# Moving a shared expert's first products into an attention loop's last steps, with the loads reordered and the results written by rows

## The chip, the cores and the metric

One Trainium2 chip, one of its cores. The time is device microseconds of one execution. Engines: PE is TensorE (PEld its weight loads), DVE is VectorE, ACT is ScalarE, POOL is GpSimd, SP is SyncE, which issues most DMAs.

## What is computed

A Perceiver layer in float32: cross attention from 32 x 64 latent rows to 32 x 1601 context rows, a span attention among the 64 rows, and a feed-forward with a shared expert and hashed experts. All residual.

```python
x = x + xattn(layernorm(x), ctx, ctx, mask)     # (32, 64, 256), 16 heads of 16, 1601 keys
x = x + span_attn(layernorm(x))                 # scores = -softplus(s1) * (pos - 64*sigmoid(s0))**2
x = x + ffn(layernorm(x))

# ffn, xf of (2048, 256)
shared = silu(xf @ sw1 + sb1) * (xf @ sw3 + sb3) @ sw2 + sb2      # 256 -> 512 -> 256
for k in range(2):                                                # two experts a row
    exp_ids = (arange(2048) * 11 + k * 7919) % 8                  # fixed by the row's number
    out += gelu(xf @ w1[e] + b1[e]) @ w2[e] + b2[e]               # 256 -> 256 -> 256
y = (shared + out / 2) / 2
```

The expert of a row depends on its number modulo 8 alone, so rows are treated in 8 classes `r`, each with two known experts.

## The kernel before

**Half batches.** The loop runs over 64 half batches `n`: batch `b = n // 2`, and half `c` of the heads. For each, TensorE makes scores `psc` (L454) in four groups of key chunks, VectorE adds the mask and puts them into `prob` (L463), and VectorE keeps a running maximum `mrun` in PSUM (L484). The maxima are turned by TensorE (`pm`, L491), reduced (`mc`, L498), turned back (`pb`, L506) and copied by ScalarE (`mb`, L510). GpSimd subtracts them from each of four pairs of heads (`less_maxima`, L515), ScalarE takes the exponential (L520), TensorE multiplies with the values into `pvs` (`values`, L530). `prob` has five slots, so that one half batch's scores are written while the last one's are read. Half batch `n` makes the scores of `n + 1`, and the projections of keys and values of the next batch (`pk` L419, `pv` L435) fill TensorE in between. In the last two half batches, 62 and 63, there is no next batch to project, and in 63 no next scores.

**The tile's steps.** Two batches make a tile of 128 rows. After its attention, `finish_steps` divides by the sums (`pr`, `rin`, `oT`), and `span_steps` does the output product `po`, the span attention and the norm ahead of the feed-forward. Its steps are taken out of an `agenda`, one in each of the loop's stretches: norm, transposes `tr_h`, `psp` and `pval`, the polynomial that ends in `mean` and `soft`, `sc` minus `mean` (L258), square, times `soft` (L263), minus `least` (L267), exponential, by `total` (L273), transposes `psa` (L281) copied to `aT`, products `po2` and `po3`, norm, and the transposed rows `xfT` (L312), from which all of the feed-forward reads. `x_kept` keeps the rows in DRAM for the last addition.

**Order.** PE, DVE, ACT and POOL run the loop in the order of the program (`manual_schedule`). What comes after `order.close()` is ordered by the scheduler, and its instructions can be put among the loop's last ones. SP and the DMAs it issues are ordered by the scheduler too. Every engine runs its instructions in order, and an instruction that waits holds those behind it. `mm_bank` hands out six PSUM banks in turn.

**The feed-forward.** After the loop the pools of the attention are closed, and the weights are loaded into their memory (L685). The shared expert's first products `p1`, `p3` (L725) run over four quarters of the rows by four chunks of the hidden width: 16 units of 8 matmul instructions each, with a Silu on ScalarE (L729) and the gated product on VectorE (L730). The last tile's steps run among the first 12; quarter 3 needs that tile. Then, class by class, `expert_hidden` makes `ph` (L748) and Gelu, and `expert_out` sums shared and expert terms in `py` (L766), with channels on the partitions. Biases are added as columns (`yT`, L770). At the end `yT` is transposed back (`pf`, L783), `x` is added (L785), and 16 tiles are stored (L786).

Of the kernel before, what the change touches and what calls it, by code (L numbers as in the profile page):

```python
# [53 lines left out]
B_2 = B_1 + 2 * E  # L54
B_S2 = B_2 + TOPK * 2 * E
B_V = B_S2 + 2
# [22 lines left out]
def perceiver_kernel(ctx: ExitStack, tc: tile.TileContext, a: dict[str, bass.AP], out: bass.AP):  # L79
# [13 lines left out]

    def mm_bank(name: str):
        return ps_mm.tile([P, 512], F32, tag="mm", name=name)
# [3 lines left out]
    nc.sync.dma_start(out=cst, in_=a["consts"])  # L99
# [6 lines left out]
    nc.sync.dma_start(out=cols, in_=a["cols"])  # L106
# [11 lines left out]
    load_x(0)  # L118

    def load_square(name: str, width: int = D):  # L120
        w = const.tile([P, 2, width], F32, name=f"{name}_sb")
        nc.scalar.dma_start(out=w, in_=a[name].rearrange("(c p) o -> p c o", p=P))
        return w

    wqT, wkT, wvT = (load_square(n) for n in ("wqT", "wkT", "wvT"))
    bo_row = const.tile([P, D], F32, name="bo_row")
    nc.scalar.dma_start(out=bo_row, in_=a["bo"].partition_broadcast(P))
    woP = const.tile([P, 4, D], F32, name="woP_sb")
    nc.scalar.dma_start(out=woP, in_=a["woP"])
    wspanT = load_square("wspanT", 2 * H)  # L130
    wvalT = load_square("wvalT")
    woutT = load_square("woutT")

# [183 lines left out]
    xattn = ExitStack()  # L317
    big = xattn.enter_context(tc.tile_pool(name="big", bufs=2))
# [7 lines left out]
    with tc.tile_pool(name="mask8", bufs=1) as mp:  # L326
        m8 = mp.tile([P, NKC, S], U8, name="m8")
        nc.sync.dma_start(out=m8[:CHUNK], in_=a["maskT"])
        nc.vector.tensor_scalar(madd[:CHUNK], m8[:CHUNK], -MASKED, MASKED, ALU.mult, ALU.add)
        nc.vector.tensor_scalar(  # L330
            madd[:CHUNK, NKC - 1, :], madd[:CHUNK, NKC - 1, :], cst[:CHUNK, C_PAD : C_PAD + 1],
            None, ALU.add,
        )
# [3 lines left out]
    prob = big.tile([P, 5, 2, NKC, P], F32, name="prob", bufs=1)  # L337
# [29 lines left out]
    cts: dict[int, list] = {}  # L367
# [31 lines left out]
    def load_context(b: int):  # L399
        cts[b] = []  # L400
        for g, (c0, n) in enumerate(GROUPS):
            k0, kn = c0 * CHUNK, min(n * CHUNK, KEYS - c0 * CHUNK)
            ct = big.tile([P, 2, 4 * CHUNK], F32, tag="ct", bufs=5, name=f"ct_{b}_{g}")
            nc.sync.dma_start(
                out=ct[:, :, :kn],
                in_=a["ctxT"][b].rearrange("(c p) k -> p c k", p=P)[:, :, k0 : k0 + kn],
            )
            cts[b].append(ct)
        if b % 2 == 0 and b // 2 + 1 < NTILE:
            t = b // 2 + 1  # L410
            load_x(t)
# [101 lines left out]
    def less_maxima(n: int, j: int, m):  # L513
        sj = pair_of(n, j)
        nc.gpsimd.tensor_tensor(  # L515
            sj, sj, m[:CHUNK, j, None, :].to_broadcast([CHUNK, NKC, P]), ALU.subtract
        )
# [4 lines left out]
    def values(n: int, r: int):  # L522
# [3 lines left out]
        for k in range(NKC):  # L526
            kn = min(CHUNK, KEYS - k * CHUNK)
            for j in range(4):
# [6 lines left out]
                )  # L535

# [43 lines left out]
    load_context(0)  # L580
    queries = query_steps(0)
    for _ in range(4):
        next(queries)
    for g in range(len(GROUPS)):
        project_keys(0, 0, g)
    for g in range(len(GROUPS)):
        scores(0, g, BETWEEN[g])
        if g == 0:
            first_maxima(0)
        project_keys(0, 1, g)  # L590
# [14 lines left out]
    for n, (b, c) in enumerate(halves):  # L605
# [12 lines left out]
        for g in range(len(GROUPS)):  # L618
            if g == 0:
# [13 lines left out]
            if g == 0:  # L633
                project(project_keys, c, 0)
                m = maxima_along_rows(turned[1])
                if n:
# [16 lines left out]
            less_maxima(n, g, m)  # L653
            run(4 * n + g)
            if g == 0 and n < last:
                first_maxima(n + 1)
# [12 lines left out]
    run(stretch)  # L669
    stretch += 1  # L670
# [7 lines left out]
    ps_mm = ctx.enter_context(tc.tile_pool(name="ps_mm", bufs=3, **psum))  # L678
    aside = mm_bank
    ps_y = ctx.enter_context(tc.tile_pool(name="ps_y", bufs=2, **psum))  # L680
    ps_h = ctx.enter_context(tc.tile_pool(name="ps_h", bufs=3, **psum))
# [6 lines left out]
    sw1 = load_weights("sw1_sb", 2, HS, a["sw1"])  # L688
    sw3 = load_weights("sw3_sb", 2, HS, a["sw3"])
    gT = ffn.tile([P, NHC, E, CL], F32, name="gT")  # L690
    sw2 = load_weights("sw2_sb", NHC, D, a["sw2"])
    w1, w2 = [], []
    for e in range(E):
        w1.append(load_weights(f"w1_{e}", 2, D, a["w1"][e]))
        w2.append(load_weights(f"w2_{e}", 2, D, a["w2"][e]))

    nc.gpsimd.tensor_tensor(sw2, sw2, sw2, ALU.add)
    ybias = ffn.tile([P, 2 * E], F32, name="ybias")
    nc.vector.tensor_tensor(
        ybias, cols[:, B_2 : B_2 + 2 * E], cols[:, B_2 + 2 * E : B_2 + 4 * E], ALU.add  # L700
    )
    for c in range(2):
        for _ in range(2):
            nc.vector.tensor_scalar(
                ybias[:, c * E : (c + 1) * E], ybias[:, c * E : (c + 1) * E],
                cols[:, B_S2 + c : B_S2 + c + 1], None, ALU.add,
            )
    nc.vector.tensor_scalar(ybias, ybias, 0.25, None, ALU.mult)

    QL = CL // 4
    for quarter in range(4):
        at = slice(quarter * QL, (quarter + 1) * QL)
        if quarter == 3:
            while agenda:
                run(stretch)
                stretch += 1
        for hc in range(NHC):
            hs = slice(hc * P, (hc + 1) * P)  # L720
            p1 = ps_h.tile([P, E, QL], F32, tag="h", name=f"p1_{quarter}_{hc}")
            p3 = ps_h.tile([P, E, QL], F32, tag="h", name=f"p3_{quarter}_{hc}")
            for ps, w in ((p1, sw1), (p3, sw3)):
                for c in range(2):
                    nc.tensor.matmul(  # L725
                        ps, lhsT=w[:, c, hs], rhs=xfT[:, c, :, at], start=(c == 0), stop=(c == 1)
                    )
            act = hid.tile([P, E, QL], F32, tag="act", name=f"act_{quarter}_{hc}")
            nc.scalar.activation(act, p1, AF.Silu, bias=cols[:, B_S1 + hc : B_S1 + hc + 1])  # L729
            nc.vector.scalar_tensor_tensor(  # L730
                gT[:, hc, :, at], p3, cols[:, B_S3 + hc : B_S3 + hc + 1], act, ALU.add, ALU.mult
            )
            run(stretch)
            stretch += 1

    yT = ffn.tile([P, 2, NT], F32, name="yT")
    xe = ffn.tile([P, NTILE, D], F32, name="xe")
    nc.sync.dma_start(out=xe, in_=x_kept.rearrange("t p d -> p t d"))
    yTr = yT.rearrange("p c (i r) -> p c r i", r=E)
# [19 lines left out]
    def expert_out(r: int, hids):  # L759
        py = ps_y.tile([P, 2, CL], F32, tag="y", name=f"py_{r}")  # L760
        for m in range(2):
            ms = slice(m * P, (m + 1) * P)
            terms = [(sw2[:, hc, ms], gT[:, hc, r, :]) for hc in range(NHC)]
            terms += [(w2[e][:, c, ms], hT[:, c, :]) for e, hT in hids for c in range(2)]
            for n, (w, x) in enumerate(terms):
                nc.tensor.matmul(  # L766
# [85 lines left out]
```

## Time and profile before

| | |
|---|---|
| median of 3 runs | 1680.48 us (1679.57 to 1681.05) |
| the profiled execution | 1680.07 us |
| its span, first to last instruction | 1678.3 us |
| mean granted TensorE clock | 0.988 |
| busy: PE, DVE, ACT, POOL | 1585.9, 1305.6, 911.3, 1105.9 us |

How to read it: all times in a view count from the start of the span. A window line gives the length, then busy microseconds and instructions of each engine, the granted TensorE clock, the share of the DMA engines and GB/s. A timeline line gives start, duration, engine, line, operation, out<-in, shape, count, and in brackets how long the engine had stood idle and what released it; several like instructions in a row are one line. A float32 matmul of the program is two instructions in these counts.

### The profile page before, as it was taken

How to read it: one execution, taken by the hardware profiler on the slowest of the kernel's cores; microseconds unless marked ns; L12 is line 12 of the kernel's file. 1: busy time of each engine (PE TensorE's matmuls, PEld its weight loads, DVE VectorE, ACT ScalarE, POOL GpSimd, SP SyncE). 2: the span in 40 equal slices, each digit the busy share in tenths (PEclk: the TensorE clock that was granted, in tenths of full speed). 3: DMA queues.
4: the chain of work that ended last, by engine and by line, in shares of the span. 5: the costliest groups of instructions: out<-in, count | busy, mean ns of one | idle time of the engine just before them, and what ended most of it. 6: DMA issues, size and time to landing. Idle time of an engine off the chain costs nothing.

```text
span 1678.3 us, 55766 instructions
## 1 busy us (share of the span) xinstructions
PE 1585.9 (94%) x25160; PEld 1192.8 (71%) x25160; DVE 1305.6 (78%) x2637; ACT 911.3 (54%) x1271; POOL 1105.9 (66%) x395
## 2 busy tenths in 40 slices
PE   6999999999999999999999999999999999859998
PEld 4777777777777777777777777777777777644586
DVE  4788988887888889888888888897889888873112
ACT  2555656565656656565656666555656565534210
POOL 0767767787686877677877868786768777672000
PEclk9999999999999999999999999999999999969999
DMA  4211111111111111111111111111111111003101
GB/s 131 58 40 42 33 40 40 38 42 48 41 42 47 41 36 33 41 39 38 41 48 41 42 48 41 39 38 39 37 43 32 45 42 32 2 26 117 54 0 51
DMA packets 51789, 72.50 MB, mean 43 GB/s; under 512 B 3684, under 2 KB 50912, under 8 KB 51552
## 3 DMA queue, kind: packets, MB, share of 16 engines
q1 hardware_dynamic: 49632, 66.95, 13.9%
q8 instruction: 197, 3.23, 0.8%
q10 hardware_dynamic: 1920, 2.00, 0.3%
q14 instruction: 40, 0.33, 0.1%
HBM read 64.74 MB, written 4.19 MB: 41 GB/s over the span
## 4 chain that ended last, share of the span: by engine, by line
PE 55%; DVE 38%; issue 3%; POOL 1%; DMA 1%; ACT 1%; POOLq 0%; ACTq 0%; DVEq 0%
DVE prob L463 13%; DVE mrun L484 13%; PE pk L419 12%; PE pv L435 12%; PE pvs L530 9%; PE psc L454 8%; PE py L766 3%; DVE rin L557 3%; PE p L725 2%; PE pm L491 2%; PE ph L748 2%; PE pb L506 1%; DVE least L266 1%; DVE mrun L251 1%; DVE total L271 1%
## 5 line engine op out<-in xcount | busy, mean ns | idle before, releaser
L515 POOL TENSOR_TENSOR prob<-prob,mb 124x1664 f32<-124x1664 f32 x256 | 950.3, 3731 | 330.4 <-ACT mb L510 330.4
L463 DVE TENSOR_TENSOR prob<-psc,madd 124x384 f32<-124x384 f32 (+1 forms) x1024 | 584.5, 584 | 188.7 <-PE psc L454 188.7
L484 DVE TENSOR_TENSOR mrun<-prob,mrun 124x512 f32<-124x512 f32 x704 | 484.1, 688 | 7.2 <-ACT mrun L476 4.3
L419 PE MATMUL pk<-ct,wkT_sb 128*128 128x372 f32 (+2 forms) x1024 | 406.1, 520 | 8.7 <-DVE prob L463 0.2
L520 ACT ACTIVATE prob<-prob 124x1664 f32<-124x1664 f32 x256 | 400.0, 1587 | 14.7 <-POOL prob L515 14.3
L435 PE MATMUL pv<-wvT_sb,ct 128*124 128x256 f32 (+1 forms) x1664 | 384.6, 379 | 0.0
L435 PEld LDWEIGHTS pv<-wvT_sb,ct 128*124 128x124 f32 (+1 forms) x1664 | 309.9, 186 | 77.3 <-DVE prob L463 2.4
L454 PE MATMUL psc<-qbd,kT 32*124 32x128 f32 x6656 | 298.5, 287 | 33.8 <-DVE prob L463 29.0
L423 ACT ACTIVATE kT<-pk,cols 128x372 f32<-128x372 f32 (+2 forms) x256 | 152.1, 594 | 293.8 <-PE pk L419 293.4
L454 PEld LDWEIGHTS psc<-qbd,kT 32*124 32x124 f32 x6656 | 235.3, 182 | 107.1 <-DVE prob L463 55.5
L419 PEld LDWEIGHTS pk<-ct,wkT_sb 128*128 128x128 f32 x1024 | 174.3, 190 | 112.0 <-issue 29.6
L441 ACT COPY v<-pv 124x512 f32<-124x512 f32 (+1 forms) x224 | 124.7, 557 | 215.4 <-PE pv L435 214.1
L530 PE MATMUL pvs<-prob,v 124*17 124x64 f32 x13312 | 216.0, 222 | 3.7 <-ACT prob L520 3.7
L530 PEld LDWEIGHTS pvs<-prob,v 124*17 124x17 f32 x13312 | 193.2, 99 | 29.4 <-issue 24.8
L770 DVE TENSOR_SCALAR yT<-py,ybias 128x256 f32<-128x256 f32 x16 | 10.9, 679 | 74.1 <-PE py L766 74.1
L725 PE MATMUL p<-xfT,sw_sb 128*128 128x512 f32 x128 | 58.7, 616 | 2.8 <-DMA sw_sb<-in_sw 1.4
L557 DVE RECIPROCAL rin<-pr 128x256 f32<-128x256 f32 x32 | 56.0, 1750 | 5.8 <-PE pr L553 5.8
L506 PEld LDWEIGHTS pb<-cst,mc 128*124 128x124 f32 x256 | 29.8, 135 | 35.9 <-DVE mc L498 30.1
L491 PE MATMUL pm<-cst,mx 124*128 124x124 f32 x256 | 40.7, 282 | 9.8 <-DVE mx L484 8.9
L725 PEld LDWEIGHTS p<-xfT,sw_sb 128*128 128x128 f32 x128 | 24.9, 198 | 33.8 <-issue 28.4
L484 DVE TENSOR_TENSOR mx<-prob,mrun 124x512 f32<-124x512 f32 x64 | 44.0, 687 | 2.2
L156 POOL TENSOR_TENSOR rstd_f<-ve_f,neghalf 128x1 f32<-128x1 f32 x16 | 8.8, 549 | 55.4 <-DVE ve_f L154 55.4
(138 smaller groups left out, 1224.7 us busy)
## 6 DMA issues: line engine op xcount, KB each, us to landing
ct<-in_ctxT SPq DMA_DIRECT2D x64, 372.0 KB, 3.2
ct<-in_ctxT SPq DMA_DIRECT2D x32, 496.0 KB, 3.6
ct<-in_ctxT SPq DMA_DIRECT2D x32, 361.0 KB, 3.1
w<-in_w SPq DMA_DIRECT2D x16, 256.0 KB, 7.1
x<-in_x SPq DMA_DIRECT2D x16, 128.0 KB, 2.0
x_kept<-x SPq DMA_DIRECT2D x16, 128.0 KB, 1.7
xe<-x_kept SPq DMA_DIRECT2D x1, 2048.0 KB, 8.2
out<-ot SPq DMA_DIRECT2D x16, 128.0 KB, 1.8
```

Of the source, the lines that this page charges most:

```text
L419: nc.tensor.matmul(ps[:, :kn], lhsT=wkT[:, i, c * P : (c + 1) * P], rhs=cts[b][g][:, i, :kn], start=(i == 0), stop=(i == 1),)
L423: nc.scalar.activation(kTs[c][:, k0 : k0 + kn], ps[:, :kn], AF.Identity, bias=cols[:, B_K + c : B_K + c + 1])
L435: nc.tensor.matmul(ps[:kn, n * D : (n + 1) * D], lhsT=cts[b][g][:, i, k0 : k0 + kn], rhs=wvT[:, i, :], start=(i == 0), stop=(i == 1),)
L441: nc.scalar.copy(vs[b % 2][:kn, 2 * u : 2 * u + n, :, :DK], ps[:kn, : n * D].rearrange("p (n h d) -> p n h d", n=n, d=DK),)
L454: nc.tensor.matmul(ps[:CHUNK, k * P : (k + 1) * P], lhsT=kTs[c][32 * j : 32 * j + 32, at : at + CHUNK], rhs=qbd[b // 2][32 * j : 32 * j + ...
L463: nc.vector.tensor_tensor(pair_of(n, j)[:, c0 : c0 + nb, :].rearrange("p k (e q) -> p k e q", e=2), ps[:CHUNK, : nb * P].rearrange("p (k e ...
L484: nc.vector.tensor_tensor(dst, block_of(n, k), run, ALU.max)
L515: nc.gpsimd.tensor_tensor(sj, sj, m[:CHUNK, j, None, :].to_broadcast([CHUNK, NKC, P]), ALU.subtract)
L520: nc.scalar.activation(pair_of(n, j), pair_of(n, j), AF.Exp)
L530: nc.tensor.matmul(pvs[32 * j : 32 * j + DK + 1, c, r, :], lhsT=v[:kn, k, 8 * c + h, :], rhs=pair_of(n, h // 2)[:kn, k, (h % 2) * S : (h % ...
L557: nc.vector.reciprocal(rin, pr[:, : 4 * S])
L725: nc.tensor.matmul(ps, lhsT=w[:, c, hs], rhs=xfT[:, c, :, at], start=(c == 0), stop=(c == 1))
```

## The change

- The first loads change places: on the ACT queue `wkT`, `wqT`, `wvT` alone; on SP the first piece of context, `x`, the constants, and the other pieces, with all other weights behind. `sw1` and `sw3` are loaded here too and stay. The program makes the four key products in turn with the query's steps.
- `prob` moves to a pool that is kept, and gated products, biases and residual rows of the feed-forward lie in its slots.
- A `unit` (two products, 8 matmul instructions) and its `gate` (Silu, gated product) are functions now. Units 0 to 2 run in half batch 62, 3 and 4 in 63, 5 to 11 among the last tile's steps, 12 to 15 after them.
- In half batch 63 `less_maxima` runs on VectorE instead of GpSimd.
- The second products have rows on the partitions: `py` takes the gated or hidden values as the stationary operand and the weights as the moving one. Biases come as rows: `b2row`, broadcast to all partitions, is summed into `brow` and from there into the residual rows `xe[r]`, by GpSimd. `yT`, the transposes and `ybias` go. Each `py` has one VectorE instruction and one store of 128 rows, eight apart.

```diff
+    wkT = load_square("wkT", nc.scalar)
+    load_piece(0, 0)
     load_x(0)
-    wqT, wkT, wvT = (load_square(n) for n in ("wqT", "wkT", "wvT"))
+    nc.sync.dma_start(out=cst, in_=a["consts"])
+    nc.sync.dma_start(out=cols, in_=a["cols"])
+    wqT = load_square("wqT", nc.scalar)
+    load_piece(0, 1)
+    load_piece(0, 2)
+    wvT = load_square("wvT", nc.scalar)
+    m8 = big.tile([P, NKC, S], U8, name="m8", bufs=1)
+    nc.sync.dma_start(out=m8[:CHUNK], in_=a["maskT"])
+    load_piece(0, 3)
...
+    woutT = load_square("woutT", nc.sync)
+    sw1 = load_square("sw1", nc.sync, HS)
+    sw3 = load_square("sw3", nc.sync, HS)
+    load_x(1)
...
-    def less_maxima(n: int, j: int, m):
+    def less_maxima(n: int, j: int, m, engine):
         sj = pair_of(n, j)
-        nc.gpsimd.tensor_tensor(
+        engine.tensor_tensor(
...
+    spare = prob.rearrange("p a b k q -> p a (b k q)")
+    REGION = E * 2 * QL
+
+    def region(h: int, hc: int):
+        a0, n = ((3, hc), (4, hc))[h] if hc < 3 else (0, h)
+        return spare[:, a0, n * REGION : (n + 1) * REGION].rearrange("p (r i) -> p r i", r=E)
...
+    def unit(u: int):
+        quarter, hc = divmod(u, NHC)
+        slot = slice(quarter * QL, (quarter + 1) * QL)
+        pair = []
+        for name, w in (("p1", sw1), ("p3", sw3)):
+            ps = mm_bank(f"{name}_{u}")
+            for c in range(2):
+                nc.tensor.matmul(
+                    ps, lhsT=w[:, c, hc * P : (hc + 1) * P], rhs=xfT[:, c, :, slot],
+                    start=(c == 0), stop=(c == 1),
+                )
+            pair.append(ps)
+        waiting.append((u, *pair))
+
+    def gate():
+        u, p1, p3 = waiting.popleft()
...
+        nc.scalar.activation(act, p1, AF.Silu, bias=cols[:, B_S1 + hc : B_S1 + hc + 1])
+        nc.vector.scalar_tensor_tensor(
+            gated_at(quarter, hc), p3, cols[:, B_S3 + hc : B_S3 + hc + 1], act, ALU.add, ALU.mult
+        )
...
-    for _ in range(4):
-        next(queries)
     for g in range(len(GROUPS)):
         project_keys(0, 0, g)
+        next(queries)
...
         for g in range(len(GROUPS)):
+            if waiting and n < last:
+                gate()
...
                 m = maxima_along_rows(turned[1])
+                if n == last:
+                    unit(3)
...
-            less_maxima(n, g, m)
+            less_maxima(n, g, m, nc.vector if n == last else nc.gpsimd)
             run(4 * n + g)
+            if n == last - 1 and g < 3:
+                unit(g)
+            if n == last and g == 1:
+                gate()
+                unit(4)
...
+    begin = {1: 5, 4: 6, 7: 7, 9: 8, 10: 9, 12: 10, 16: 11}
+    gated = {1: 1, 4: 1, 7: 1, 9: 1, 10: 1, 12: 1, 14: 1}
+    for s in range(19):
+        run(stretch + s)
+        for _ in range(gated.get(s, 0)):
+            gate()
+        if s in begin:
+            unit(begin[s])
+    for u in range(3 * NHC, 4 * NHC):
+        unit(u)
+        gate()
+    gate()
     order.close()
     xattn.close()
...
+    b2row = ffn.tile([P, E + 1, D], F32, name="b2row")
+    nc.sync.dma_start(out=b2row, in_=a["b2"].partition_broadcast(P))
 
     nc.gpsimd.tensor_tensor(sw2, sw2, sw2, ALU.add)
...
+    brow = spare[:, 2, 4 * D : (4 + E) * D].rearrange("p (r d) -> p r d", r=E)
+    for r in range(E):
+        nc.gpsimd.tensor_tensor(
+            brow[:, r, :], b2row[:, expert_of(0, r), :], b2row[:, expert_of(1, r), :], ALU.add
+        )
+    for _ in range(2):
+        nc.gpsimd.tensor_tensor(
+            brow, brow, b2row[:, None, E, :].to_broadcast([P, E, D]), ALU.add
+        )
+    nc.gpsimd.tensor_scalar(brow, brow, 0.25, None, ALU.mult)
...
+    for r in range(E):
+        x2 = spare[:, 1 + r // 6, r % 6 * 2 * D : (r % 6 + 1) * 2 * D]
+        xe.append(x2.rearrange("p (h d) -> p h d", h=2))
+        nc.sync.dma_start(out=xe[r], in_=kept_rows[r])
+        nc.gpsimd.tensor_tensor(
+            xe[r], xe[r], brow[:, r, None, :].to_broadcast([P, 2, D]), ALU.add
+        )
...
+        for h in range(2):
+            py = ps_y.tile([P, D], F32, tag="y", name=f"py_{r}_{h}")
+            hs = slice(h * P, (h + 1) * P)
+            terms = [(region(h, hc)[:, r, :], sw2[:, hc, :]) for hc in range(NHC)]
+            terms += [(hT[:, c, hs], w2[e][:, c, :]) for e, hT in hids for c in range(2)]
+            for n, (x, w) in enumerate(terms):
+                nc.tensor.matmul(py, lhsT=x, rhs=w, start=(n == 0), stop=(n == len(terms) - 1))
+            ot = hid.tile([P, D], F32, tag="ot", bufs=4, name=f"ot_{r}_{h}")
+            nc.vector.scalar_tensor_tensor(ot, py, 0.25, xe[r][:, h, :], ALU.mult, ALU.add)
+            nc.sync.dma_start(out=out_rows[r, h], in_=ot)
...
-    for t in range(NTILE):
-        ps = mm_bank(f"pf_{t}")
-        for c in range(2):
-            nc.tensor.transpose(ps[:, c * P : (c + 1) * P], yT[:, c, t * P : (t + 1) * P], ident)
-        ot = hid.tile([P, D], F32, tag="ot", bufs=4, name=f"ot_{t}")
-        nc.vector.tensor_tensor(ot, xe[:, t, :], ps[:, :D], ALU.add)
-        nc.sync.dma_start(out=out[t * P : (t + 1) * P, :], in_=ot)
```

## The prediction

> **What bounds the kernel now.** I read the slices of the page first, then the windows of both ends, then the timelines around the joints. From about 40 to 1455 us TensorE is above 90% and the compiled order of instructions there is the same before and after, so this stretch can only shift as a whole. The change acts on the first 20 us and on everything after 1455 us. The windows of the end:
>
> ```profile
> core 0: us, PE busy (x) PEld busy (x) DVE busy (x) ACT busy (x) POOL busy (x), PEclk, DMA share, GB/s
> 1465.00:1475.00 10.00, 7.07 (x79) 5.46 (x83) 9.72 (x17) 5.47 (x5) 10.00 (x4) 0.57 0.01 2
> 1485.00:1495.00 10.00, 2.63 (x98) 2.45 (x87) 8.68 (x6) 4.40 (x4) 9.66 (x4) 0.67 0.01 2
> 1580.30:1665.50 85.20, 84.43 (x387) 72.30 (x386) 10.94 (x16) 13.77 (x33) 0.00 (x0) 1.00 0.00 1
> 1665.50:1678.30 12.80, 6.10 (x32) 2.99 (x30) 7.05 (x17) 0.00 (x0) 0.00 (x0) 0.85 0.49 165
> ```
>
> In half batch 62 (1455 to 1481) VectorE is the full engine, in 63 (1481 to 1506) GpSimd; TensorE idles in both, at a clock near 0.6. The experts (1580 to 1665) are TensorE alone. The last 12.8 us are output only. The joints, from the timeline:
>
> ```profile
> 14.73 6.02 PE L419 MATMUL pk<-ct,wkT_sb 128*128 128x496 f32 x16
> 20.68 1.15 PE L454 MATMUL psc<-qbd,kT 32*124 32x128 f32 x32
> ...
> 1511.42 0.51 ACT L162 ACTIVATE xn_f<-x,neg_f 128x256 f32<-128x256 f32 x1 [3.87 <-DVE neg_f L152]
> 1511.94 1.28 ACT L729 ACT_TABLE_LOAD   x1
> 1513.24 0.69 ACT L729 ACTIVATE act<-p,cols 128x512 f32<-128x512 f32 x1
> ...
> 1543.98 1.90 POOL L273 TENSOR_TENSOR sc<-sc,total 128x1024 f32<-128x1024 f32 x1 [2.77 <-DVE total L272]
> 1556.47 1.04 PE L281 MATMUL psa<-cst,sc 128*128 128x128 f32 x8
> ```
>
> First scores start at 20.68 us. The last tile's softmax is ready at 1545.88, but `psa` sits behind shared-expert matmuls until 1556.47. From `psa` a serial chain (aT, po2, po3, norm, `xfT`) runs to 1563.97; then quarter 3 takes 16.4 us, part of it at half clock, and the experts start at 1580.33.
>
> I keep the clock of this execution for all steps and take the shift of the start off at the end. Its own time is 1680.07 us around a span of 1678.30; the median of the runs is 1680.48, 0.02% away.
>
> **1. Start.** The keys' weights (256 KB) and the first piece of context (496 KB) now lead their queues. The windows show 11 GB/s in the first 2 us, then 248, then 367. With `x`, `cst` and `wqT` beside them 1.3 MB are in by about 5.3 us, and all 2.9 MB up to the fourth piece by 2.3 + 7.8 = 10.1 us. So the first key product runs at 5.3 instead of 14.73. The compiled order is three key pieces, `tr_q`, the fourth, `pq`, scores; ScalarE puts the second key copy ahead of `xn_q`. I get `xn_q` at 10.6 to 11.7, `tr_q` 11.8, fourth piece to 13.4, `pq` to 15.2 (1.8 us; 2.07 in the timeline), two of the four `qbd` copies (0.37 each) to 16.0, with slack 16.4. Gain 20.68 − 16.4 = 4.3. If bytes come at the 241 to 258 GB/s of 6 to 10 us it is about 2; if only the bytes bind, 6. The bulk loads (sw1, sw3, woP and others, 2.3 MB) come behind and are in by about 19; their first reader is `pbv`, 32.28 before.
>
> **2. Half batch 62: units 0 to 2.** A unit is 8 matmuls of 0.43 us (3.43), one Silu (0.69) and one gated product on VectorE (0.75). TensorE has the room; VectorE and ScalarE pay. Gate 0 stands on VectorE ahead of the additions of scores group 1, and its Silu stands on ScalarE behind the copy `mrun`, which waits for `soft`: 1464.99 + 0.59 + table load 1.28 + 0.69 = 1467.55. VectorE, free at 1464.9, adds only at 1468.35 instead of 1464.82: +3.5. Gate 1 falls into the wait for `rin`'s bank: +0.6. Gate 2: Silu at 1478.3, hidden under the additions, product +0.75. Sum +5.0; the maxima `mx` end at 1486.5. The queue behind each gate is group 1, 2 or 3 of the additions, and TensorE waits for those banks.
>
> Here a rule is weighed. The row: the load at 1511.94 is followed by its ACTIVATE 1.30 us later. The Trainium skill (ScalarE: Activation LUTs, What ACT_TABLE_LOAD costs) adds a drain of about 1.38 us to each switch of set. By the rule gate 0 costs 1.4 more, and gate 2, behind five switches (exp, Silu, exp, Silu after the first), some 6.4 more; the stage would be +11, not +5. I take the row.
>
> **3. Half batch 63: subtraction to VectorE, units 3 and 4.** GpSimd's four (3731 ns each, 14.8 us) leave, and its `sc` step no longer stands between them. On VectorE, from 512 to 1664 elements at the 1.03 ns per element between its 384 (551 ns) and 512 rows (683 ns), one takes about 1.88 us. `pm`, `mc`, `pb`, `mb` end at 1490.3; two subtractions to 1494.1, `total` and its reciprocal to 1495.6, gate 3 to 1496.8, two more. What is late next is ScalarE: Silu 3 with two table loads (3.3), exponentials 0 and 1 to 1498.2, then `aT` of tile 14, which waits for `psa`, behind units 3 and 4 on TensorE (to about 1502), then exponentials 2 and 3 to 1506.4. Values end at 1508.1 instead of 1506.3: these two half batches together cost +1.8, for five units done.
>
> A second rule speaks against this move: the Trainium skill (SBUF — State Buffer, SBUF: two separate sides) has a VectorE instruction with two SBUF inputs and a GpSimd instruction lock each other out for a whole instruction. The trace shows such a hold:
>
> ```profile
> L704 DVE TENSOR_SCALAR ybias<-ybias,cols x4: 1945/3680/3757, 1489.1 to 1498.2; 128x8 f32<-128x8 f32 x4
> L708 DVE TENSOR_SCALAR ybias<-ybias x1: 176/176/176, 1502.0 to 1502.0; 128x16 f32<-128x16 f32 x1
> ```
>
> Eight elements take as long as GpSimd's subtraction, and 176 ns once it is done. In half batch 63 one GpSimd instruction meets the subtractions, `sc` by `total` (1.9 us): the third waits some 0.8 us beyond gate 3. By rows alone they end at 1500.6, with the hold at 1501.4; ScalarE is later than both, so the sum is the same. The old kernel's `ybias` (14 us on VectorE) was off the path and gives nothing.
>
> **4. From the last values to the experts.** Before: 1506.3 to 1580.33, with 16 units. Now 11 units. The weights are in the constant pool, so `po` no longer waits behind unit 0 and the 3.71 us load: `oT` 1511.4, `po` to 1513.2, `ve_h` 1514.7. `rstd_h` stands on GpSimd behind the doubling of `sw2` (1.89, to 15.5), as before: `xn_h` at 1516.9. Unit 5 ends at 1516.7, `tr_h` follows, `psp` at 1517.7 instead of 1526.11, `z` at 1522.4 after vbd, Silu 5 and a load, `mean` 1524.6, `sc` minus `mean` to 1526.6, square to 1527.7, times `soft` to 1529.6.
>
> Now the costly part. GpSimd's compiled order puts four sums of `b2row` before `sc` minus `least`, and four more and the two 128x2048 additions before `sc` by `total`. Rows: 128x256 0.73 us; 128x1664 3.73 us with the same kind of operand, so 2048 about 4.57 (from 128x1024, 1.91 with a column operand, it would be 3.8). Then 2.9 us before `least` is subtracted (to 1534.4), exponential to 1535.5, reciprocal to 1537.1; on GpSimd 2.9 + 9.1 more from 1534.4 to 1546.5, and only then `sc` by `total`, to 1548.4. Units 6 to 10 end at 1536.4 (five times 3.43 from 1519.2), so TensorE idles 12 us, and I give it half clock on waking, as at 1563.97 (0.86 us per matmul for 5 us): `psa` to 1550.4, po2 and po3 to 1554.4, unit 11 to about 1559.5, `tr_f`, `xfT`, units 12 to 15 from 1560.3 to 1574.0 (13.7). The first `ph` waits on VectorE, I take it for the last gate's bank: +0.9. Experts at 1574.9 instead of 1580.33. Stage: 66.8 instead of 74.0, −7.2. Without the bias sums on this path it would be −18.
>
> `b2row` (1.2 MB) is queued behind x_kept of tile 14 (1511.8) and ten weights at 0.84 us apart, so lands about 1526; GpSimd asks at 1529.6. Covered by 3 us, no more.
>
> **5. Experts.** Same matmuls by kind and number (384), the operands of `py` changed round. 384 x 0.2155 = 82.8. The 0.3 us waits of `py` for `yT` vanish with four banks: 85.1 becomes 83.0, −2.1. Reading residuals by rows: eight 256 KB loads issue at about 1555, 2 MB in about 8 us, eight GpSimd sums of about 1.2; done by 1568, first needed after 1582. Covered.
>
> **6. Output.** Transposes and 16 additions with 4 `ot` buffers: 1665.45 to 1678.30, 12.85. After: one 128x256 product (0.45) and, from the end of the last addition to the end of the span, the same 2.69: 3.2. −9.65. The other 15 stores (1.8 us, every 1.7) lie under the experts.
>
> **Sum.** −4.3 + 1.8 − 7.2 − 2.1 − 9.65 = −21.4. 1680.07 − 21.4 = 1658.6; against the median 1659.0.
>
> **Rivals.**
> (a) As worked out: 1651 to 1667, for the start by ±2, ScalarE and half clock by ±3, GpSimd's sums by ±3. 0.80.
> (b) GpSimd's sums hide after all, because they are cheaper or `psa` was later anyway: `psa` near 1538 to 1541, 8 to 11 us less: 1640 to 1651. For it: TensorE is then full all through. Against: the order is fixed and 14 us of sums lie in it. 0.11.
> (c) The products in the half batches cost what they save: the drain of the rule in stage 2, or units 1 and 2 at half clock (PEclk is 0.57 there now), which delays gate 2 by 4. The rule's drains make +6.4 in stage 2 and +2.8 (two switches) in stage 3; with the half clock +13: 1663 to 1672. The change would then not do what it says there. Beyond 1667: 0.06.
> (d) Slower than before: `b2row` lands late. GpSimd waits for it with `least` and `total` behind, and TensorE behind those. It is a broadcast of nine rows to 128 partitions, and no load here has that size and form (bo_row, 128 KB, took 5.8 us in a crowd). Every us past 1529.6 is a us; from 1551, that is 30 us after issue, the gain is gone. At 35 us after issue it is 1685. 0.03.
>
> **Numbers.** 1659; 1651 to 1667 holds 0.80 by (a). Faster by over 0.2% (3.4 us, about what this measurement can tell from no change) in (a), (b), (c) and little else: 0.96; same 0.01; slower 0.03.
>
> **What would show it.** First scores near 16.4 us; in half batch 62 the Silu of unit 0 ending about 2.6 us after `soft`, with VectorE idle before its product; exponential 2 of half batch 63 behind `aT`; GpSimd busy with the `b2row` sums between exponential and `sc` by `total`, TensorE idle over 8 us before the last `psa`, half clock after; the last `py` followed by the end within 3.5 us. Wrong: an early `psa`, a GpSimd wait on a DMA, experts longer than 85 us.

## The result, and the profile after

The changed kernel takes 1655.09 us (median of 4 runs, 1654.66 to 1656.14) where the kernel before took 1680.03 us beside it: ratio 0.9854, 95% interval 0.9836 to 0.9871. Predicted were 1659.0 us and 1651 to 1667. The profiled execution took 1654.66 us, its span is 1652.9 us (before 1678.3), the mean granted TensorE clock 0.993.

The 25.4 us between the two spans, by stage, read from the timelines at the same events:

| stage | before, us | after, us | change | predicted |
|---|---|---|---|---|
| start to the first `psc` | 20.68 | 16.02 | -4.7 | -4.3 |
| from there to half batch 62 (first values of 61) | 1434.38 | 1433.75 | -0.6 | 0 |
| half batches 62 and 63, to the end of the last values | 51.21 | 50.47 | -0.7 | +1.8 |
| to the first `ph` | 73.90 | 66.21 | -7.7 | -7.2 |
| experts, to the end of the last `py` | 85.28 | 83.15 | -2.1 | -2.1 |
| output | 12.85 | 3.30 | -9.6 | -9.65 |

Further down, half batch 62 is counted from the end of the last half batch's maxima `mx` to the end of its own, and 63 from there to the end of the last values. By this measure 62 went from 24.4 to 29.0 us and 63 from 24.8 to 19.5.

First the windows of the kernel after, at the places that answer to the four shown of before:

```profile
core 0: us, PE busy (x) PEld busy (x) DVE busy (x) ACT busy (x) POOL busy (x), PEclk, DMA share, GB/s
1460.00:1470.00 10.00, 8.59 (x63) 4.36 (x63) 7.65 (x13) 9.88 (x10) 10.00 (x4) 1.00 0.01 2
1481.00:1490.00 9.00, 8.23 (x104) 4.59 (x108) 6.19 (x6) 4.31 (x5) 0.30 (x1) 0.67 0.00 0
1566.40:1649.60 83.20, 83.15 (x384) 72.88 (x384) 6.37 (x15) 13.44 (x32) 0.00 (x0) 1.00 0.07 24
1649.60:1652.90 3.30, 0.00 (x0) 0.00 (x0) 0.42 (x1) 0.00 (x0) 0.00 (x0) 1.00 0.12 40
```

In half batch 62 (first line) TensorE works 8.6 of 10 us at full clock, where it had 7.1 at 0.57; ScalarE is now as full as GpSimd. In 63 (second line) GpSimd is nearly empty. The experts are TensorE without a gap. Behind them come one addition of 0.42 us and a store.

The start, from the timeline after:

```profile
5.65 6.24 PE L434 MATMUL pk<-ct,wkT_sb 128*128 128x496 f32 x12 [5.65 <-DMA wkT_sb<-in_wkT]
12.29 0.44 PE L198 MATMUL tr_q<-cst,xn_q 128*128 128x128 f32 x2 [0.41 <-ACT xn_q L191]
16.02 1.15 PE L469 MATMUL psc<-qbd,kT 32*124 32x128 f32 x32 [0.90 <-ACT qbd L412]
```

The key products come first, at 5.65 us (predicted 5.3), the first scores at 16.02 (predicted 16.4).

Then the last tile's softmax, timeline after:

```profile
1524.99 1.90 POOL L295 TENSOR_TENSOR sc<-sc,least 128x1024 f32<-128x1024 f32 x1
1526.85 2.78 POOL L780 TENSOR_TENSOR prob<-b2row 128x256 f32<-128x256 f32 x4
1529.27 0.25 DVE L300 RECIPROCAL total<-total 128x16 f32<-128x16 f32 x1
1529.70 9.07 POOL L784 TENSOR_TENSOR prob<-prob,b2row 128x2048 f32<-128x2048 f32 x2
1538.73 1.90 POOL L301 TENSOR_TENSOR sc<-sc,total 128x1024 f32<-128x1024 f32 x1
1540.68 1.97 PE L309 MATMUL psa<-cst,sc 128*128 128x128 f32 x8 [11.48 <-POOL sc L301]
```

The reciprocal is there at 1529.52, but two additions of a bias, 4.5 us each, stand next in GpSimd's order and begin at 1529.70; `sc` by `total` waits 9.2 us behind them, and TensorE stands for 11.48 us. This is the largest wait that the change leaves, and the first thing to test.

### The profile page after: what moved, and what is told of

The parts are those of the page before. It is cut to its first block, busy times and chain, and to the rows that moved or that the text cites. A ratio compares the mean times of both kernels' runs of the same rounds, so it can differ in the third digit from the quotient of the medians.

```text
span 1652.9 us, 55724 instructions
## 1 busy us (share of the span) xinstructions
PE 1572.0 (95%) x25128; PEld 1182.3 (72%) x25128; DVE 1288.4 (78%) x2619; ACT 921.0 (56%) x1279; POOL 1120.8 (68%) x410
## 4 chain that ended last, share of the span: by engine, by line
PE 57%; DVE 38%; issue 2%; POOL 1%; ACT 1%; DMA 0%; ACTq 0%; DVEq 0%; POOLq 0%
DVE prob L478 13%; DVE mrun L499 13%; PE pk L434 13%; PE pv L450 13%; PE pvs L545 9%; PE psc L469 8%; PE py L826 3%; DVE rin L615 3%; PE p L575 2%; PE pm L506 2%; PE ph L808 2%; PE pb L521 1%; DVE mrun L279 1%; DVE least L294 1%; PE pval L236 1%
## 5 line engine op out<-in xcount | busy, mean ns | idle before, releaser
L530 POOL TENSOR_TENSOR prob<-prob,mb 124x1664 f32<-124x1664 f32 x252 | 935.3, 3730 | 326.7 <-ACT mb L525 326.7
L469 PE MATMUL psc<-qbd,kT 32*124 32x128 f32 x6656 | 294.6, 286 | 30.6 <-DVE prob L478 26.0
L545 PE MATMUL pvs<-prob,v 124*17 124x64 f32 x13312 | 211.3, 219 | 1.8 <-ACT prob L535 1.8
L545 PEld LDWEIGHTS pvs<-prob,v 124*17 124x17 f32 x13312 | 188.8, 98 | 27.5 <-issue 25.2
L828 DVE SCALAR_TENSOR_TENSOR ot<-py,prob 128x256 f32<-128x256 f32 x16 | 6.8, 424 | 76.9 <-PE py L826 76.9
L506 PE MATMUL pm<-cst,mx 124*128 124x124 f32 x256 | 40.7, 282 | 10.4 <-DVE mx L499 9.4
L815 ACT ACTIVATE hT<-ph,cols 128x256 f32<-128x256 f32 x32 | 13.4, 471 | 57.4 <-PE ph L808 57.4
```

Source lines behind the costliest of these rows:

```text
L469: nc.tensor.matmul(ps[:CHUNK, k * P : (k + 1) * P], lhsT=kTs[c][32 * j : 32 * j + 32, at : at + CHUNK], rhs=qbd[b // 2][32 * j : 32 * j + ...
L530: engine.tensor_tensor(sj, sj, m[:CHUNK, j, None, :].to_broadcast([CHUNK, NKC, P]), ALU.subtract)
L545: nc.tensor.matmul(pvs[32 * j : 32 * j + DK + 1, c, r, :], lhsT=v[:kn, k, 8 * c + h, :], rhs=pair_of(n, h // 2)[:kn, k, (h % 2) * S : (h % ...
```

## The experiments

All were timed beside the kernel before. "Faster than before" is the difference of the medians of one session; an interval of a ratio is 0.0012 to 0.0019 to each side, 2 to 3 us. The changed kernel is 24.9 us faster than before by this measure. It, e1 to e4, e5 to e8 and e9 to e12 were timed in four sessions, so a difference between two of these has an error of about 3 us (an estimate from the two intervals); what is smaller is read from the stages. Stage lengths come from one profile each. Identical code up to half batch 62 ended in them within about 2 us, so stages are compared, not absolute times.

| run | median, us | before beside it | faster than before | ratio, 95% interval |
|---|---|---|---|---|
| e1 sums behind | 1642.1 | 1679.44 | 37.3 | 0.9779 (0.9766 to 0.9792) |
| e2 subtraction on GpSimd | 1661.07 | 1679.44 | 18.4 | 0.9894 (0.9879 to 0.9909) |
| e3 old start | 1658.66 | 1679.44 | 20.8 | 0.9878 (0.9864 to 0.9891) |
| e4 units last | 1673.29 | 1679.44 | 6.2 | 0.9965 (0.9952 to 0.9977) |
| e5 units last, on e1 | 1658.29 | 1680.81 | 22.5 | 0.9874 (0.9855 to 0.9892) |
| e6 no Silu table, on e1 | 1639.88 | 1680.81 | 40.9 | 0.9755 (0.9742 to 0.9768) |
| e7 late gate, on e1 | 1641.08 | 1680.81 | 39.7 | 0.9763 (0.9750 to 0.9776) |
| e8 combined, on e1 | 1645.16 | 1680.81 | 35.7 | 0.9792 (0.9778 to 0.9805) |
| e9 units shifted, on e1 | 1637.34 | 1678.74 | 41.4 | 0.9750 (0.9737 to 0.9764) |
| e10 exponentials first, on e1 | 1641.66 | 1678.74 | 37.1 | 0.9780 (0.9767 to 0.9793) |
| e11 tail chain, on e1 | 1639.1 | 1678.74 | 39.6 | 0.9762 (0.9749 to 0.9776) |
| e12 orders of e9, e10, e11 | 1634.53 | 1678.74 | 44.2 | 0.9736 (0.9723 to 0.9749) |

**e1: the bias sums behind the softmax.** The hand-written order ends later, so that the sums keep their place in the program:

```diff
     gate()
-    order.close()
     xattn.close()
...
     nc.gpsimd.tensor_scalar(brow, brow, 0.25, None, ALU.mult)
+    order.close()
```

> GpSimd's sums of b2row (eight 128x256, two 128x2048, one scaling) and the doubling of sw2 stand behind the last tile's last step on GpSimd instead of among its softmax steps; the order on TensorE, VectorE and ScalarE is the same. Theory (the sums hold the softmax, and the softmax holds TensorE): sc minus least comes 2.7 us earlier, sc by total some 12 us earlier, psa starts when unit 10 ends on TensorE (1529 instead of 1540.7), and since TensorE then doesn't wake from an idle of 11.5 us, psa, po2, po3 and unit 11 lose 1 to 3 us of half clock: 12 to 14 us faster than 1655, 1641 to 1643. Rival (psa is bound by something else than the sums, by the exponential or by TensorE's queue): 0 to 3 us faster. Rival (the sums only move: the rows' additions in the experts come late and VectorE makes TensorE wait for py's banks): less than 8 us faster, with waits of py on DVE.

12.4 us faster than the changed kernel (37.3 against 24.9; by the spans 13.9, by the two stages below 13.4). From the timeline of e1:

```profile
1523.10 1.90 POOL L295 TENSOR_TENSOR sc<-sc,least 128x1024 f32<-128x1024 f32 x1 [1.33 <-DVE least L294]
1527.78 1.90 POOL L301 TENSOR_TENSOR sc<-sc,total 128x1024 f32<-128x1024 f32 x1 [2.77 <-DVE total L300]
1529.73 1.09 PE L309 MATMUL psa<-cst,sc 128*128 128x128 f32 x8 [1.05 <-POOL sc L301]
1533.44 3.60 PE L575 MATMUL p<-xfT,sw_sb 128*128 128x512 f32 x8
```

From the last values to `psa` it takes 30.0 us instead of 40.4. Between `psa` and the first `ph` another 2.95 us go (22.82 instead of 25.77), with the same instructions: `psa` takes 1.09 instead of 1.97 us and unit 11 3.60 instead of 4.60. The windows tell why, first after, then e1:

```profile
1535.00:1540.00 5.00, 0.00 (x0) 0.00 (x0) 0.00 (x0) 0.00 (x0) 5.00 (x2) 0.50 0.00 0
1540.00:1545.00 5.00, 3.74 (x41) 2.90 (x42) 0.75 (x1) 2.14 (x4) 5.00 (x2) 0.50 0.02 3
```

```profile
1530.00:1535.00 5.00, 4.21 (x48) 2.75 (x47) 2.00 (x6) 2.03 (x5) 0.00 (x0) 1.00 0.03 8
```

After 11.5 us without work TensorE wakes at half clock; after 1.05 us it does not. That agrees with the Trainium skill (TensorE: Matmul & The Clock Gate, Part 1: The HAM clock gate), which has the clock fall to half after an idle window of about 3.4 us. Two later profiles show a fall behind shorter idles as well (2.3 us ahead of the last `psa` in e5; e11 below), which that rule does not give. So the wait costs 10.4 us and its echo 3. The sums themselves are as long as before and now lie beside units 12 to 15 and the first experts; no `py` or `ot` waits for them.

**e2: subtraction back to GpSimd.**

```diff
-            less_maxima(n, g, m, nc.vector if n == last else nc.gpsimd)
+            less_maxima(n, g, m, nc.gpsimd)
```

> The four subtractions of the maxima in half batch 63 go back to GpSimd, units 0 to 4 stay where they are. Theory (GpSimd was what half batch 63 ran by): they take 4 x 3.73 us with a 1.9 us sc step between, against 3.69 + 5.10 us on VectorE: 5 to 6 us slower than 1655, about 1660.5. Rival (ScalarE, with the exponentials behind aT and the Silu tables, sets the end of half batch 63): under 2 us slower.

6.5 us slower, near the 5 to 6 expected. Half batch 63 takes 24.94 instead of 19.47 us. GpSimd runs two subtractions, `sc`, two subtractions, and the exponentials follow it. From the timeline of e2:

```profile
1483.84 7.39 POOL L530 TENSOR_TENSOR prob<-prob,mb 124x1664 f32<-124x1664 f32 x2 [3.79 <-ACT mb L525]
1491.19 1.91 POOL L301 TENSOR_TENSOR sc<-sc,total 128x1024 f32<-128x1024 f32 x1
1493.05 7.38 POOL L530 TENSOR_TENSOR prob<-prob,mb 124x1664 f32<-124x1664 f32 x2
```

On VectorE in the changed kernel the same four take 1.89 us each, except one that meets GpSimd's `sc` by `total` and takes 3.30. That hold (1.4 us) fits the rule on the two sides of SBUF that the prediction weighed, and it is smaller than the gain.

**e3: the old start.** Loads and steps of the start in the old order, `sw1` and `sw3` last.

```diff
-        project_keys(0, 0, g)
         next(queries)
+    for g in range(len(GROUPS)):
+        project_keys(0, 0, g)
```

> Loads and steps of the start in the order of the kernel before, all else as changed. Theory: first scores again at about 20.7 instead of 16.0 us, and the shift stays to the end: 4.7 to 5.3 us slower than 1655, about 1660. Rival (the steady stretch has slack that takes up a late start): under 2 us slower.

4.1 us slower (span 4.7). The first scores come at 22.1 us, 6.1 later; the maxima of half batch 62 end 6.1 later; so the steady stretch takes up nothing. (22.1 us is 1.4 later than in the kernel before, since the key products took 7.17 us instead of 6.02; why they did is open.) 1.1 us come back just before the experts: here the first `ph` does not wait for the last gate, as it does in the changed kernel (0.91 us).

**e4 and e5: units 0 to 4 behind units 12 to 15.** The call of unit 3, the first entry of `gated` and the place of the Silu's result change too and are left out here.

```diff
-            if n == last - 1 and g < 3:
-                unit(g)
-            if n == last and g == 1:
-                gate()
-                unit(4)
...
-    for u in range(3 * NHC, 4 * NHC):
+    for u in [*range(3 * NHC, 4 * NHC), *range(5)]:
```

> Units 0 to 4 taken out of the last two half batches and put behind units 12 to 15, so that TensorE does them alone, full speed, 3.43 us each. Theory (TensorE had room there and the units cost only VectorE's and ScalarE's time): half batch 62 gets its 4.6 us back, half batch 63 some 2 to 4, the tail grows by 5 x 3.43 = 17.2: 9 to 11 us slower than 1655, about 1665. Rival (the units cost in the half batches what they save): within 2 us of 1655.

18.7 us slower, more than either theory has. Half batch 62 is 4.6 us shorter (24.41), half batch 63 not at all (19.78 against 19.47), and between the last values and `psa` 6.7 us were added, most of which had nothing to do with units. From the timeline of e4:

```profile
1526.52 9.09 POOL L775 TENSOR_TENSOR prob<-prob,b2row 128x2048 f32<-128x2048 f32 x2
1535.69 5.37 POOL L778 TENSOR_SCALAR prob<-prob 128x2048 f32<-128x2048 f32 x1
1541.04 1.90 POOL L301 TENSOR_TENSOR sc<-sc,total 128x1024 f32<-128x1024 f32 x1
1543.00 1.97 PE L309 MATMUL psa<-cst,sc 128*128 128x128 f32 x8 [18.12 <-POOL sc L301]
```

The compiler had put the scaling, 5.37 us, ahead of `sc` as well: what is not in the written order can land elsewhere after an edit. The other 1.3 us stand ahead of `mean`, and e5 has them too. So the test was made again on the kernel of e1, where it is fixed:

> As e4 (units 0 to 4 behind units 12 to 15), but on the kernel of e1, where GpSimd's order is fixed and the sums of b2row cannot move into the softmax chain; the kernel to compare with is e1 (1642.1). In e4 half batch 62 gave back 4.5 us, half batch 63 nothing, and 6.6 us came only from 5.4 us of GpSimd's scaling that the compiler put ahead of sc by total. Theory (half batch 63 hides units 3 and 4 wholly, half batch 62 charges 4.5 us for units 0 to 2): 17.2 - 4.5 = 12.7 us slower than e1, about 1654.8. Rival (units in the half batches cost what they save): within 2 us of e1.

14.8 us slower than e1 (22.5 against 37.3). The execution that was profiled took 1666.75 us, 8.5 more than the median, and its maxima came 10.9 us later than in e1 already ahead of half batch 62, so only stage lengths are used: half batch 62 -4.6 us, 63 -0.2, to `psa` +1.3, from `psa` to `ph` +18.7. Of the last, 17.2 are the five units; the rest is half clock again (`po3` 2.08 us, unit 11 5.05 us). Five units in the half batches therefore save some 15 us after their price, which is 4.6, all of it in half batch 62. Rival (c) is out; units 1 and 2 did not run at half clock there either (3.70 us each; the window from 1460 to 1470 has a granted clock of 1.00).

**e6: no Silu table in the half batches.** On e1; the gates of units 0 to 3 leave Silu out.

```diff
-        nc.scalar.activation(act, p1, AF.Silu, bias=cols[:, B_S1 + hc : B_S1 + hc + 1])
+        nc.scalar.activation(act, p1, AF.Silu if u > 3 else AF.Identity, bias=cols[:, B_S1 + hc : B_S1 + hc + 1])
```

> On the kernel of e1, the gate of units 0 to 3 uses the identity with bias instead of Silu, so that ScalarE stays with one table through half batches 62 and 63; this leaves the Silu of these four units out. Theory by the row (a switch costs its 1.28 us load and nothing more): the wait of VectorE before gate 0 shrinks from 2.7 to 1.4, and half batch 63's exponentials start 2.6 us earlier but still have aT between them: 1.3 to 2.5 us faster than e1 (1642.1), 1639.6 to 1640.8. Rival by the rule (each switch drains 1.4 us more, with seven or eight switches in the two half batches): over 4 us faster, below 1638. Rival (tables hidden): within 0.5 us of e1.

3.6 us faster than e1 by the medians, which alone would not part the three forecasts; 1.1 us of it is the wait of the first `ph`, which this build does not have. Half batch 62 is 1.5 us shorter (27.47), by VectorE's wait before gate 0, now 1.33 us instead of 2.71; half batch 63 is no shorter (20.21 against 19.87), since `psa` is held by TensorE. The first gate in the timeline of the changed kernel (the wait is 2.71 us in e1 too), then of e6:

```profile
1460.30 1.28 ACT L590 ACT_TABLE_LOAD   x1
1461.60 0.69 ACT L590 ACTIVATE prob<-p,cols 128x512 f32<-128x512 f32 x1
1462.32 0.75 DVE L591 SCALAR_TENSOR_TENSOR prob<-p,cols,prob 128x512 f32<-128x512 f32 x1 [2.71 <-ACT prob L590]
```

```profile
1461.44 0.68 ACT L590 ACTIVATE prob<-p,cols 128x512 f32<-128x512 f32 x1
1462.16 0.75 DVE L591 SCALAR_TENSOR_TENSOR prob<-p,cols,prob 128x512 f32<-128x512 f32 x1 [1.33 <-ACT prob L590]
```

The load starts 0.02 us after the copy ahead of it ends (1460.28), and the Silu 1.30 us later; without the load the wait is 1.38 us shorter, where a load and a drain would make 2.66. Eight switches of table in the two half batches cost 1.2 us together, about one load. The drain of 1.38 us for each, by the rule weighed in the prediction, is not there.

**e7: the gates later.** On e1, in half batch 62 a gate follows the additions of its group.

```diff
-            if waiting and n < last:
-                gate()
...
                 scores(n + 1, g, BETWEEN[g])
+                if waiting:
+                    gate()
```

> On the kernel of e1, in half batch 62 each gated product stands behind the additions and maxima of its scores group instead of ahead of them. Theory (VectorE's 2.7 us wait for Silu 0 is what half batch 62 pays beyond the three products of 0.75 us): 2.7 us faster than e1 (1642.1), about 1639.4. Rival (units' banks are then held longer and TensorE's scores wait for them, so that VectorE gets its next group later): within 1 us of e1, or slower.

2.4 us faster by the medians, near the 2.7 expected but within the error, and not for the reason given: half batch 62 takes 29.19 us, with e1 28.98. What is shorter is again the wait of the first `ph` (1.1 us) and the rest is within the error. In the timeline of e7 the wait has only changed its owner:

```profile
1456.47 3.70 PE L575 MATMUL p<-xfT,sw_sb 128*128 128x512 f32 x8
1460.10 0.94 PE L469 MATMUL psc<-qbd,kT 32*124 32x128 f32 x24
1461.06 0.56 DVE L478 TENSOR_TENSOR prob<-psc,madd 124x384 f32<-124x384 f32 x1 [1.71 <-PE psc L469]
```

TensorE is in unit 0 when VectorE comes to the scores of group 1. Of the 2.7 us only 1.0 is gone, and later waits of VectorE for scores, 0.35 and 0.80 us, which e1 does not have, take it back.

**e8: four orders at once.** On e1: late gates as in e7; in half batch 63 exponentials ahead of `aT`; all four `sc` steps of the last tile on VectorE; unit 5 ahead of `po`.

```diff
-        nc.gpsimd.tensor_tensor(
+        eng.tensor_tensor(
             sc, pos[:, None, :].to_broadcast(full), mean[:, :, None].to_broadcast(full), ALU.subtract
...
-    begin = {1: 5, 4: 6, 7: 7, 9: 8, 10: 9, 12: 10, 16: 11}
+    begin = {0: 5, 1: 6, 4: 7, 7: 8, 9: 9, 10: 10, 16: 11}
```

> The kernel of e1 and four more changes of order: the late gates of e7; in half batch 63 the exponentials ahead of aT and gate 3 behind them; the last tile's four sc steps, and the last of tile 14, on VectorE (about 1.1 us instead of 1.9); unit 5 already before po, the next units one place earlier, unit 10 last before psa. Theory (after e1, TensorE and the softmax chain are level before psa, so both must be shortened): 2.7 in half batch 62, 3 to 4 in half batch 63, 2.5 to 4 in the tail: 1632 to 1634. Rival (only one of the two is shortened, or VectorE with the subtractions and the sc step becomes what half batch 63 runs by): 1636 to 1639.

1.6 us slower than e1, against both theories. Half batch 62 gains nothing (29.20), as in e7. Half batch 63 gains 1.8 us (18.05), but from the last values to `psa` it takes 32.2 us instead of 30.0, and then half clock after an idle of 4.5 us costs 2.5. Two lines of the timeline of e8 show a part:

```profile
1518.18 0.17 DVE L275 SCALAR_TENSOR_TENSOR mean<-mrun,rden 128x16 f32<-128x16 f32 x1
1520.87 1.22 DVE L287 TENSOR_TENSOR sc<-cst,mean 128x1024 f32<-128x1024 f32 x1
```

`mean` is ready at 1518.35, and on GpSimd the next step starts at once (in e1 at 1516.80, 0.17 after `mean`). On VectorE it stands behind the polynomial for `soft` and a gate, 2.5 us. The faster engine was the busy one. And unit 5, put ahead of `po`, delays the norm and `tr_h`: 11.2 us from the last values instead of 9.1.

**e9: the units one group later.** On e1. Now TensorE's order changes with VectorE's.

```diff
-            if n == last - 1 and g < 3:
-                unit(g)
+            if n == last - 1 and g:
+                unit(g - 1)
...
                     maxima_of_rows(*turned)
+                    gate()
```

> On the kernel of e1, in half batch 62 units 0 to 2 stand one scores group later on TensorE (behind groups 1, 2 and 3 instead of ahead of them), their gates behind the additions of the next group, gate 2 at the start of half batch 63 while VectorE waits for pb. In e7 the late gate alone gained nothing, because TensorE was in unit 0 when VectorE had come to group 1. Theory (half batch 62 pays for unit 0 in the order of TensorE as well as in the wait for Silu): 2 to 4 us faster than e1 (1642.1), 1638 to 1640. Rival (VectorE, with its own work, is what half batch 62 runs by, and only the 0.75 us of gate 2 leave it): 0 to 1 us faster.

4.1 us faster than e1. Half batch 62 takes 26.63 us (-2.35), half batch 63 17.17 (-2.7), which was not expected at all. The reason is in TensorE's lines of the timeline, first e1, then e9:

```profile
1479.90 1.01 PE L506 MATMUL pm<-cst,mx 124*128 124x124 f32 x4 [5.24 <-DVE mx L499]
1482.58 5.73 PE L575 MATMUL p<-xfT,sw_sb 128*128 128x512 f32 x8
```

```profile
1479.26 0.61 PE L506 MATMUL pm<-cst,mx 124*128 124x124 f32 x4 [1.14 <-DVE mx L499]
1481.12 3.60 PE L575 MATMUL p<-xfT,sw_sb 128*128 128x512 f32 x8
```

With unit 2 at the end of half batch 62, TensorE idles 1.1 us before `pm` instead of 5.2 and keeps its clock (1.00 from 1480 to 1485, in e1 0.50): `pm`, `pb` and unit 3 run at full speed, which is 0.40, 0.46 and 2.13 us less. Of the gain in half batch 62, 0.75 us is the product of gate 2, which has moved to half batch 63.

**e10: exponentials first.** On e1, in half batch 63 all exponentials ahead of `aT`, gate 3 behind.

```diff
+            if g and n == last:
+                exponentials(n, g - 1)
+            if g == 3 and n == last:
+                exponentials(n, 3)
             run(4 * n + g)
```

> On the kernel of e1, in half batch 63 all four exponentials stand ahead of aT of tile 14 on ScalarE, and gate 3 behind them. Theory (what held the last values was ScalarE's order: exponentials 2 and 3 behind aT, aT behind psa, psa behind units 3 and 4 on TensorE): exponential 3 ends at 1495 to 1497 instead of 1498.0, and the end comes 2 to 3 us earlier than e1 (1642.1), 1639 to 1640. Rival (TensorE's queue sets the last values anyway, since values stand behind unit 4 and psa): 0 to 1 us.

No faster than e1 (37.1 and 37.3). Half batch 63 is 2.5 us shorter (17.35), as the theory has it, but 1.1 us are handed on: Silu 3 and its table load now stand ahead of the copy `o`, so that `pr` starts 1.61 us after the last values instead of 0.48. The remaining 1.4 us are within the error of the medians.

**e11: the tail.** On e1: half of unit 5 ahead of `po`, gate 5 earlier, three `sc` steps on VectorE, the first on GpSimd.

```diff
+        if s == 0:
+            unit(5, (0,))
+        if s == 1:
+            unit(5, (1,))
...
-    gated = {1: 1, 4: 1, 7: 1, 9: 1, 10: 1, 12: 1, 14: 1}
+    gated = {1: 1, 2: 1, 7: 1, 9: 1, 10: 1, 12: 1, 14: 1}
```

> On the kernel of e1, only the tail is changed: half of unit 5 fills TensorE's 1.6 us before po, gate 5 stands ahead of the copy hT, and the last three sc steps of tile 15 run on VectorE (1.2 us instead of 1.9; the first stays on GpSimd, beside the polynomial on VectorE, which e8 had put behind it: there that step started 2.5 us later). Theory (e1's TensorE and softmax chain end within 1 us of each other before psa, and both are shortened, TensorE by 1.7 and the chain by 3 to 3.6): 2.5 to 3 us faster than e1 (1642.1), 1639 to 1639.6. Rival (as in e8, an idle TensorE wakes at half clock, or VectorE's gates hold the sc steps): same as e1 or slower.

2.3 us faster, within the error; from the last values to `psa` it takes 29.68 us (e1 30.01), and 1.1 us are the first `ph` again. The softmax is ready at 1527.9, 2.5 us ahead of `psa`; what is late is TensorE, whose units 6 to 10 took 19.13 us instead of 17.43. From the windows of e11:

```profile
1511.00:1516.00 5.00, 5.00 (x17) 2.31 (x14) 1.62 (x9) 4.34 (x7) 0.00 (x0) 0.66 1.06 356
```

In this execution the granted clock fell to 0.66 there. Why it did is open: TensorE had idled only 0.7 and 0.5 us just before. The transfers in that line are no reason: e1 and e12 have a DMA share of 1.11 and 1.09 there, and a clock of 1.00.

**e12: the orders of e9, e10 and e11 together.**

> The orders of e9, e10 and e11 together on the kernel of e1. Theory (three stretches in series, each shortened by itself): the sum of what each gains, 6 to 9 us, 1633 to 1636. Rival (a stretch hands its gain on to the next as a wait): less than the largest of the three gains plus 1 us.

1634.53 us, 6.9 us faster than e1, the fastest of all, and near the sum of the three single gains (4.1, -0.2 and 2.3, by the medians). Against e1: half batch 62 -2.3, 63 -3.4, to `psa` -0.9, from there to `ph` -1.1. Here units 6 to 10 take 17.43 us again.

## Why the prediction was right, and where it was off

1. **Start**, predicted -4.3, measured -4.7. The order of loads and the queue of ScalarE were read rightly. In part it is luck: `tr_q` came 0.5 us later than written and `pq` took 1.05 us instead of 1.8, so that `pq` ended at 15.11 where the text has 15.2, and the 0.4 us between 16.02 and 16.4 are the slack that had been added. `pq` is short by its place: behind TensorE's first instructions it takes 2.07 us (before) and 2.08 (e3), behind 6 us of key products 1.05. That this is the clock is not shown, since the granted clock in the windows is 1.00 in all three. In the eleven other profiles with the same start the first `psc` is at 15.5 to 16.7 us. e3 shows that a later start comes through undiminished. That the steady stretch was 0.6 us shorter is not explained; it is inside its spread from profile to profile (1433.3 to 1434.8; e5, long there, left out).
2. **Half batch 62**, predicted +5.0, measured +4.6. The delay at gate 0, the largest term, was put at 3.5, a wait of 2.65 and a product; the wait is 2.71 and the product 0.75. e5 confirms it from the other side (-4.6 without the units). The row was taken instead of the rule of a drain, and e6 shows that it was right. What the prediction did not see is that this price has two causes in series, VectorE's wait and TensorE's own unit (e7), so that it falls only where both are moved (e9, by 1.6 us without the product of gate 2). Some 3 us are left, 2.25 of them the three products.
3. **Half batch 63**, with 62 predicted +1.8, measured -0.7; alone -3.2 and -5.3. This is the mis-sized step. The prediction had `psa` of tile 14 behind units 3 and 4 "to about 1502" in the times of the kernel before; unit 4 ends at 1494.05, which is 1499.3 in those times (5.29 us of shift, from the first values of 61). Unit 3 took 5.25 us and unit 4 only 3.70, since TensorE was back at full clock by then, as the windows of the kernel after show:

```profile
1485.00:1490.00 5.00, 5.00 (x95) 2.48 (x97) 4.97 (x5) 3.14 (x4) 0.30 (x1) 0.81 0.00 0
1490.00:1495.00 5.00, 5.00 (x60) 2.77 (x50) 5.00 (x3) 4.04 (x4) 1.60 (x1) 1.00 0.01 3
```

Exponential 3 therefore ends 2.5 us earlier than the 1506.4 of the text. The order (exponentials 2 and 3 behind `aT` behind `psa` behind the units) was right, as e10 shows. The hold by GpSimd was put at 0.8 us and is 1.4.

4. **Last values to experts**, predicted -7.2, measured -7.7. The two long sums took 9.07 us (predicted 9.1), the small ones 2.78 (2.9), TensorE idled 11.48 (12), half clock followed, and the first `ph` waited 0.91 (0.9). For a kernel without the sums on this path the text had -18; in e1 the stage takes 52.8 us, -21.1. The missing 3 us are the half clock, which goes with the idle. `b2row` was never waited for: rival (d) is out. GpSimd did wait for a DMA, which the prediction had listed as a sign of being wrong: 4.5 us in two waits for the residual rows, the last until 1555.6, but off the path: the first `py` comes after 1566.
5. **Experts**, predicted -2.1, measured -2.1.
6. **Output**, predicted -9.65, measured -9.6. No run takes 5 or 6 out alone; both are read from the timelines, where the transposes and their waits are gone. Results by rows save 11.7 us by these two stages, but they brought the sums of `b2row`, which cost 13.4 where the compiler had put them. Only with e1 does this part of the change pay.

Rival (b), that the sums hide, is refuted by e1: they cost 12 to 14. The forecast was 4 us too long because of the half batches (2.5 us), the start (0.4), the steady stretch (0.6) and the tail (0.5), all on the same side.

## What to carry to other kernels

Price a long wait of TensorE twice, as the wait and as the half-clock matmuls behind it; here 10.4 and 3 us behind an idle of 11.5, while 1.1 us of idle had no echo. In e9 a unit moved into an idle stretch shortened the half batch behind it by 2.7 us, since TensorE kept its clock. Work that is off the critical path by its data can be on it by its place in an in-order queue: fix its place in the program rather than trust the compiler, which in e4 put a scaling of 5.4 us ahead of the critical step when something else was edited. And when a stage gets shorter, look where the next stage starts: in e7 and e10 the gain was handed on as another wait.

## What the runs showed of the hardware that was not expected

- A lock works both ways. In e4, e5 and e12 VectorE's subtraction was running when GpSimd's `sc` by `total` came: the latter took 3.35 us instead of 1.90, and the pair of subtractions 5.33 us instead of 3.69. In the changed kernel GpSimd came first, took its 1.90, and one subtraction took 3.30.
- GpSimd's scaling of 128x2048 by a constant took 5.37 us, longer than the addition of two such operands (4.5 us).
- The first `ph` waited 0.91 us for the last gated product in the changed kernel, e1, e2, e8 and e10, and not at all in e3, e6, e7, e9, e11 and e12, though the order of TensorE around it is the same. The cause is open (e6 differs from e1 by one function of ScalarE alone), so that the 0.9 us of the prediction came true without being understood; 1 us of several comparisons above hangs on it.
